# Encoder-decoder layer on one core: short blocks' exponentials queued after the copies, a block's first unit turned head by head, the next rows' norm on ScalarE, and token sums in three parts

## The chip, the cores and the metric

The kernel runs on one core of a Trainium2 chip. The metric is device microseconds of one execution; the number before is the median of three runs, 2858.91 us (2858.62 to 2859.53). Engines are named as the profile names them: PE (TensorE matmul), PEld (its weight load), DVE (VectorE), ACT (ScalarE), POOL (GpSimd), SP (the queue that issues DMAs).

## What is computed

One pre-norm encoder layer on a short source (2 x 77 tokens), and one pre-norm decoder layer on 2 x 2048 tokens, width 512, 16 heads of 32, feed-forward width 2048, all float32. Cut to the decoder, where nearly all the work is:

```
y  = tgt                                   # (2, 2048, 512)
yn = ln(y, n1)
y  = y + mha(yn, yn, sa, bias = rel_self + causal)     # softmax over 16 heads
y  = y + mha(ln(y, n2), memory, ca, bias = rel_cross)  # memory: 77 tokens a batch
h  = ln(y, n3)
y  = y + relu(h @ ff1.T + b1) @ ff2.T + b2
```

`ln` is the layer norm over the 512 columns; `mha` scales scores by 1/sqrt(32), adds the bias, takes the softmax over the keys and multiplies by the values.

## The kernel before

**Blocks and units.** A batch has four blocks of 512 query rows (m = 0 to 3), eight blocks in all. In the first part of the program (to about 1750 us) each block runs its causal self-attention in 16 units: four groups g of four heads, times four tiles t of 128 query rows. A unit's number of key tiles is m*4 + t + 1, so the units of m = 0 are the short ones (1 to 4 key tiles) and those of m = 3 the long ones (13 to 16). Beside a unit run the jobs of a list by unit (`jobs`, `light`, `ahead`, `late`, lines 905 to 943): the projections of queries, keys and values, the output projection of the block before, the layer norm of the next block's rows, and, in the m = 0 block of batch 0, the whole encoder in stages; in the m = 0 block of batch 1, the cross-attention of the first block.

**A unit's steps.** `scores` (line 354) multiplies queries and keys of four heads into four PSUM banks (line 371, four heads on four row groups of the array), and DVE copies them out with a running maximum (lines 380, 387) and takes the row's negated maximum `nm` (line 397). ACT takes the exponential of each head in place and its sum (line 402); for m = 0 the four are issued at once, for m of 1 and more they are put in a list, `late_exps`, from which `exps(k)` issues k at chosen places. `turn` (line 411) transposes the 128 x 128 pieces on PE (line 425), four to a PSUM bank, and copies each bank out, half of them on DVE (line 429) and half on ACT (line 431). For m = 0 a bank holds the pieces of one head, for other blocks the pieces of four heads for one key tile. `values` (line 436) multiplies the copies with the values (line 442).

**The order of the work** is written out by hand (`manual_schedule`, the main loop of lines 1511 to 1536), and every engine runs its own list in order. For a unit n the loop issues: the scores and exponentials of n that are still missing; the norm's statistics that are due (`ahead`); `turn` of a pair of pieces of n; the next unit's list (`slot`); scores of n + 2; one or two late exponentials; `values` of the pair. The scores' banks, the transposes' banks, the jobs' banks and the norm's bank come from one ring of seven, taken in program order (`bank`, line 179).

**The norm of the next rows.** For four units in the middle of a block (lines 933 to 937), one tile a unit: `norm_stats` (bn_stats, bn_aggr, plus epsilon on DVE, the power -1/2 on POOL, lines 281 to 285), `norm_center` (subtract the mean, times rstd, on DVE, 128 x 512, line 291), and a unit later `norm_turn` (four transposes into one bank, line 303, and four 128 x 128 evictions with scale and bias on DVE, line 310). The rows of the very first block are done ahead of everything, with `apart` set, three of their four evictions on ACT (line 308).

**Feed-forward and cross-attention** (from about 1750 us). Each of the eight blocks runs 56 slots (`ff_slot`, line 1378): 28 of the first product and 28 of the second, both as seven products of quarter matrices on sums and differences of the quarters. Four differences of the normed tokens, T1 to T4, are made on POOL in `sums_n` (line 1239) in slot 0; the products (the table `ONE`, line 1173) use T2 from slot 4, T1 from slot 6, T3 from slot 8, T4 from slot 12. A generator `cross` (line 1439) runs the next block's cross-attention beside these slots: in slots 0 to 3 the statistics of its four tiles (POOL lines 743 and 744), two slots later each tile's centring on ACT (line 750) and an addition on POOL (line 751), two slots after that the transposes (line 756) and four evictions on ACT (line 759).

Of the kernel before, what the change touches and what calls it, by code (L numbers as in the profile page):

```python
# [10 lines left out]
F32 = mybir.dt.float32  # L11
AF = mybir.ActivationFunctionType
ALU = mybir.AluOpType
# [4 lines left out]
P = 128  # L18
# [4 lines left out]
HC = P // HD  # L23
# [31 lines left out]
def tile_encoder_decoder(ctx: ExitStack, tc: tile.TileContext, ins, out):  # L55
    nc = tc.nc
# [20 lines left out]
    def vec(name, i):  # L77
        c = _COL[name] + i
        return vecs[:, c : c + 1]
# [78 lines left out]
    with (  # L158
# [20 lines left out]
        def bank():  # L179

            i = count["bank"] % count["banks"]
            count["bank"] += 1
            return psum[:, i, :]

        def in_turn(what, tile):
            i = count[what] % tile.shape[1]
            count[what] += 1
            return tile[:, i, :]

        def rows4(r):  # L190
            return slice(r * HD, (r + 1) * HD)
# [85 lines left out]
        def norm_stats(b, m, t):  # L277
            x1 = xs[b, m, t]
            st = sm.tile([P, 6], F32, name="bnst", tag="bnst")
            mv = sm.tile([P, 2], F32, name="bnmv", tag="bnmv")  # L280
            nc.vector.bn_stats(st, x1)
            nc.vector.bn_aggr(mv, st)
            rs = sm.tile([P, 2], F32, name="rstd", tag="rstd")
            nc.vector.tensor_scalar_add(rs[:, 0:1], mv[:, 1:2], EPS)  # L284
            nc.gpsimd.tensor_tensor(rs[:, 1:2], rs[:, 0:1], mhalf[:, 0:1], ALU.pow)  # L285
            xs[b, m, t] = x1, mv, rs

        def norm_center(b, m, t):
            x1, mv, rs = xs[b, m, t]
            xs[b, m, t] = x1  # L290
            nc.vector.tensor_scalar(x1, x1, mv[:, 0:1], rs[:, 1:2], ALU.subtract, ALU.mult)

        def norm_turn(b, m, t, apart=False):
            xn = xs.pop((b, m, t))
            if t == 0:
                nTs[b, m] = nTt
            nT = nTs[b, m]

            pts = [bank()] * NC
            if apart:  # L300
                pts[0] = bank()
            for c in range(NC):
                nc.tensor.transpose(pts[c][:, ts(c, P)], xn[:, ts(c, P)], ident)
            for c in range(NC):
                d, pt = nT[:, c, ts(t, P)], pts[c]
                sc, bi = vec("dec_n1_s", c), vec("dec_n1_b", c)
                if apart and c:
                    nc.scalar.activation(d, pt[:, ts(c, P)], AF.Identity, bias=bi, scale=sc)
                else:
                    nc.vector.tensor_scalar(d, pt[:, ts(c, P)], sc, bi, ALU.mult, ALU.add)  # L310
# [16 lines left out]
        units = [(b, m, g, t) for b in range(B) for m in range(NMB) for g in range(NC) for t in range(TB)]  # L327
# [14 lines left out]
        def probabilities(n):  # L342
            w = (units[n][1] + 1) * MB
            at = END - HC * w if n % 2 else 0
            return [pp[:, at + r * w : at + (r + 1) * w] for r in range(HC)]

        late_exps = []

        def exps(k):

            for _ in range(min(k, len(late_exps))):
                late_exps.pop(0)[1]()

        def scores(n, k0, kn):
            b, m, g, t = units[n]
            i = m * TB + t
            if k0 == 0:
                state[n] = {
                    "p": probabilities(n),
                    "mx": sm.tile([P, HC, 8], F32, name="mx", tag="mx"),  # L360
                    "nm": sm.tile([P, HC], F32, name="nm", tag="nm"),
                    "col": 0,
                }
                if t == 0:
                    sums_of[b, m, g] = sm.tile([P, TB, HC], F32, name="sums", tag="sums")
            st = state[n]
            last = k0 + kn == i + 1
            q = qTs[b, m, g]
            banks = [bank() for _ in range(HC)]
            for r in range(HC):  # L370
                nc.tensor.matmul(  # L371
                    banks[r][:, : kn * P], q[rows4(r), ts(t, P)], kT[rows4(r), g, k0 * P : (k0 + kn) * P],
                    start=True, stop=True,
                )
            far = max(0, kn - 2) if last else kn
            col = st["col"]
            for r in range(HC):
                p, s, c = st["p"][r], banks[r], col
                if far:
                    nc.vector.tensor_scalar(  # L380
                        p[:, k0 * P : (k0 + far) * P], s[:, : far * P], 1.0, None, ALU.mult, ALU.max,
                        accum_out=st["mx"][:, r, c : c + 1],
                    )
                    c += 1
                if last:
                    w = (kn - far) * P
                    nc.vector.tensor_tensor_reduce(  # L387
                        p[:, (i + 1) * P - w : (i + 1) * P], s[:, far * P : kn * P],
                        biases[b, m, g][:, r, 2 * P - w :], 1.0, LOWEST, ALU.add, ALU.max,
                        accum_out=st["mx"][:, r, c : c + 1],  # L390
                    )
                    c += 1
            st["col"] = c
            if not last:
                return

            nc.vector.tensor_reduce(st["nm"], st["mx"][:, :, :c], AX.X, ALU.max, negate=True)  # L397
            for r in range(HC):
                p, nm, to = st["p"][r][:, : (i + 1) * P], st["nm"][:, r : r + 1], sums_of[b, m, g][:, t, r : r + 1]

                def run(p=p, nm=nm, to=to):
                    nc.scalar.activation(p, p, AF.Exp, bias=nm, accum_out=to)  # L402

                if m:
                    late_exps.append((n, run))
                else:
                    run()

        got = {}

        def turn(pieces):

            first = units[pieces[0][0]][1] == 0
            loads = []
            for n, k0, kn in pieces:
                ks = range(k0, k0 + kn)
                if first:
                    loads += [[(n, k, r) for k in ks] for r in range(HC)]
                else:
                    loads += [[(n, k, r) for r in range(HC)] for k in ks]  # L420
            for o, load in enumerate(loads):
                pt = bank()
                pts = in_turn("pts", pts_all).rearrange("p (x q) -> p x q", q=P)
                for x, (n, k, r) in enumerate(load):
                    nc.tensor.transpose(pt[:, ts(x, P)], state[n]["p"][r][:, ts(k, P)], ident)  # L425
                    got[n, k, r] = pts[:, x, :]
                w = len(load) * P
                if o % 2 if first else o >= (len(loads) + 1) // 2:
                    nc.vector.tensor_copy(pts[:, : len(load), :], pt[:, :w])  # L429
                else:  # L430
                    nc.scalar.copy(pts[:, : len(load), :], pt[:, :w])  # L431
                if o == min(3, len(loads) - 1):
                    exps(1)
            exps(1)

        def values(n, k0, kn):
            b, m, g, t = units[n]
# [473 lines left out]
        for x, (b, m) in enumerate(blocks):  # L911
            u = x * NU
            first = m == 0
# [172 lines left out]
        gp, ve = nc.gpsimd, nc.vector  # L1086
# [14 lines left out]
        def minus(engine, out, a, b):  # L1101
            engine.tensor_tensor(out, a, b, ALU.subtract)  # L1102
# [130 lines left out]
        def of_n(name):  # L1233
            if name[0] == "T":
                return n_sums[:, int(name[1]) - 1]
            r, c = int(name[0]) - 1, int(name[1]) - 1
            return nTt[:, 2 * r : 2 * r + 2, ts(c, TOK)]

        def sums_n():
            minus(gp, of_n("T1"), of_n("12"), of_n("11"))  # L1240
            minus(gp, of_n("T2"), of_n("22"), of_n("T1"))
            minus(gp, of_n("T3"), of_n("22"), of_n("12"))
            minus(gp, of_n("T4"), of_n("21"), of_n("T2"))


        sets = [[high[:, (4 * a + k) * D : (4 * a + k + 1) * D] for k in range(4)] for a in range(2)]
# [130 lines left out]

        def ff_slot(s):
            x, n = divmod(s, per)
            if n == 0:  # L1380
                sums_n()
            k = n - FIRST + 4
            if 0 <= k < 4 * len(TWO):
                sums_h(k // 4, k % 4)
            if n < FIRST:
                first_product(n)
            else:
                second_product(x, (n - FIRST) // 4, (n - FIRST) % 4)
            feed(used[0] + len(w_ring))
            after.pop(s, lambda: None)()  # L1390
            if FIRST <= n < FIRST + TB:
                new_y(x + 2, n - FIRST)
# [118 lines left out]
        while i < len(stream):  # L1511
            n = stream[i][0]
# [91 lines left out]
```

## Time and profile before

| | before |
|---|---|
| median of three runs | 2858.91 us |
| the profiled execution | 2861.14 us, of which 2859.2 us from its first to its last instruction |
| PE busy | 2811.5 us (98%), 25950 matmuls |
| DVE, ACT, POOL busy | 1924.1 us (67%), 1395.4 us (49%), 782.0 us (27%) |
| chain that ended last | PE 89%, DVE 4%, ACT 3%, POOL 2% |
| mean granted PE clock | 0.991 of full speed |

A matmul's record lasts longer than the distance to the next one's start, so a PE that is busy in the table may still stand behind a wait; the distance between starts in the timeline shows it. Lines of the form "L425 <- ACT pp L402" name who ended a wait, and a number in square brackets is the time that the engine stood idle before a row.

### The profile page before, as it was taken

The page shows a single profiled execution, that of the slowest core. Times are in us where ns is not written, and L with a number is a line of the kernel's source. Part 1 is how long each engine was busy: PE and PEld are TensorE (multiplying, and loading weights), DVE is VectorE, ACT ScalarE, POOL GpSimd, SP SyncE. Part 2 cuts the span into 40 slices and gives each one's busy share as a digit, 9 for nine tenths or more (in the row PEclk, how much of TensorE's full clock was granted, in tenths as well). Part 3 has the DMA queues.
Part 4 walks back from the last instruction along what each step waited for, and adds up shares of the span by engine and source line. Part 5 has one row for each costly group of instructions (what it writes and reads, how often), then busy time and mean ns, then how long its engine had stood idle before and what let it go on. Part 6 is the DMA issues. An engine that isn't in the chain of part 4 may idle for free.

```text
span 2859.2 us, 65017 instructions
## 1 busy us (share of the span) xinstructions
PE 2811.5 (98%) x25950; PEld 2070.5 (72%) x25950; DVE 1924.1 (67%) x5416; ACT 1395.4 (49%) x2639; POOL 782.0 (27%) x669
## 2 busy tenths in 40 slices
PE   9899999999999999999999999999999999999998
PEld 5557666666666556666666677888888888888888
DVE  4667688878987677788878885464545555555545
ACT  3344455556666446555556676434344434344431
POOL 0100050200000201120100002282838383737355
PEclk9899999999999999999999999999999999999999
DMA  6413343401112411232401014464647464645466
GB/s 171 117 36 123 120 140 100 122 20 30 36 47 67 118 49 57 82 101 68 123 20 32 24 55 145 151 198 118 199 122 200 139 190 126 188 133 185 119 203 192
DMA packets 252641, 319.10 MB, mean 112 GB/s; under 512 B 29568, under 2 KB 142512, under 8 KB 252210
## 3 DMA queue, kind: packets, MB, share of 16 engines
q1 hardware_dynamic: 252338, 314.93, 37.1%
q8 instruction: 205, 3.36, 0.5%
q14 instruction: 98, 0.80, 0.1%
HBM read 274.91 MB, written 39.95 MB: 110 GB/s over the span
## 4 chain that ended last, share of the span: by engine, by line
PE 89%; DVE 4%; ACT 3%; POOL 2%; issue 1%; DMA 1%; SPq 0%; POOLq 0%; DVEq 0%; ACTq 0%
PE psum L425 17%; PE psum L1346 11%; PE psum L1317 11%; PE psum L371 11%; PE psum L442 9%; PE psum L215 4%; PE psum L239 4%; PE psum L828 4%; PE psum L251 4%; PE psum L226 3%; PE psum L1419 3%; PE psum L811 2%; PE psum L781 1%; ACT pp L402 1%; PE psum L819 1%
## 5 line engine op out<-in xcount | busy, mean ns | idle before, releaser
L402 ACT ACTIVATE pp<-pp,nm 128x128 f32<-128x128 f32 (+15 forms) x512 | 611.9, 1201 | 264.2 <-DVE nm L397 263.9
L380 DVE TENSOR_SCALAR_CACHE_REDUCE pp<-psum 128x512 f32<-128x512 f32 (+3 forms) x1024 | 559.4, 591 | 61.7 <-PE psum L371 60.2
L425 PEld LDWEIGHTS psum<-ident,pp 128*128 128x128 f32 x4352 | 477.2, 142 | 111.1 <-DVE pp L380 51.3
L425 PE MATMUL psum<-ident,pp 128*128 128x128 f32 x4352 | 540.1, 279 | 8.7 <-DVE mx L387 3.8
L431 ACT COPY pts<-psum 128x512 f32<-128x512 f32 (+3 forms) x592 | 297.9, 574 | 471.3 <-PE psum L425 376.8
L429 DVE COPY pts<-psum 128x512 f32<-128x512 f32 (+2 forms) x544 | 330.0, 660 | 69.4 <-PE psum L425 69.1
L371 PE MATMUL psum<-kT,q 32*128 32x512 f32 (+3 forms) x2560 | 362.3, 579 | 6.9 <-ACT pts L431 4.3
L442 PEld LDWEIGHTS psum<-pts,vv 128*32 128x32 f32 x8704 | 227.3, 110 | 125.7 <-issue 117.3
L1346 PEld LDWEIGHTS psum<-pp 128*128 128x128 f32 x2560 | 295.8, 192 | 17.4 <-issue 11.4
L1346 PE MATMUL psum<-pp 128*128 128x128 f32 x2560 | 306.4, 276 | 1.9 <-POOL pp L1102 1.6
L442 PE MATMUL psum<-pts,vv 128*32 128x128 f32 x8704 | 280.7, 276 | 0.7 <-ACT pts L431 0.5
L1102 POOL TENSOR_TENSOR pp<-pp 128x512 f32<-128x512 f32 x155 | 209.7, 1370 | 120.0 <-DMA pp<-in_dec_ff_wT_dram 100.4
L1317 PE MATMUL psum<-vv,pp 128*128 128x256 f32 x1024 | 238.5, 381 | 0.0
L371 PEld LDWEIGHTS psum<-kT,q 32*128 32x128 f32 x2560 | 125.1, 184 | 143.6 <-issue 88.5
L1317 PEld LDWEIGHTS psum<-vv,pp 128*128 128x128 f32 x1024 | 189.8, 190 | 26.3 <-issue 1.9
L387 DVE CUSTOM_DVE_ANT_0 pp<-psum,bias 128x256 f32<-128x256 f32 (+1 forms) x512 | 196.0, 411 | 16.3 <-PE psum L371 16.3
L285 POOL TENSOR_TENSOR rstd<-rstd,mhalf 128x1 f32<-128x1 f32 x32 | 18.2, 570 | 664.3 <-DVE rstd L284 664.3
L1330 DVE TENSOR_TENSOR kT<-kT,psum 128x512 f32<-128x512 f32 x96 | 65.7, 686 | 194.4 <-PE psum L1317 193.9
L1317 PE MATMUL psum<-nT,pp 128*128 128x256 f32 x768 | 173.4, 379 | 0.0
L1333 ACT ACTIVATE kT<-kT,vecs 128x256 f32<-128x256 f32 x192 | 86.9, 500 | 167.9 <-DVE kT L1330 167.8
L1317 PEld LDWEIGHTS psum<-nT,pp 128*128 128x128 f32 x768 | 145.3, 190 | 22.6 <-issue 3.5
L805 POOL TENSOR_TENSOR oT<-oT,cri 128x1232 f32<-128x1232 f32 x28 | 67.7, 2418 | 283.3 <-DVE cri L800 258.4
(191 smaller groups left out, 3712.3 us busy)
## 6 DMA issues: line engine op xcount, KB each, us to landing
pp<-w_d SPq DMA_DIRECT2D x520, 256.0 KB, 3.0
pp<-in_dec_ff_wT_dram SPq DMA_DIRECT2D x112, 256.0 KB, 3.8
wqk<-in_dec_sa_in_wT_dram SPq DMA_DIRECT2D x64, 256.0 KB, 4.0
bias<-tzg SPq DMA_DIRECT2D x128, 128.0 KB, 3.7
wbig<-in_dec_sa_in_wT_dram SPq DMA_DIRECT2D x8, 1024.0 KB, 6.6
vv<-in_enc_ff_wT_dram SPq DMA_DIRECT2D x8, 1024.0 KB, 5.5
wbig<-in_dec_sa_out_wT_dram SPq DMA_DIRECT2D x8, 1024.0 KB, 6.6
vv<-y SPq DMA_DIRECT2D x32, 256.0 KB, 5.8
```

Of the source, the lines that this page charges most:

```text
L215: nc.tensor.matmul(mm, w[:, c, :], nTs[b, m][:, c, :], start=(c == 0), stop=(c == NC - 1))
L371: nc.tensor.matmul(banks[r][:, : kn * P], q[rows4(r), ts(t, P)], kT[rows4(r), g, k0 * P : (k0 + kn) * P], start=True, stop=True,)
L380: nc.vector.tensor_scalar(p[:, k0 * P : (k0 + far) * P], s[:, : far * P], 1.0, None, ALU.mult, ALU.max, accum_out=st["mx"][:, r, c : c + 1],)
L387: nc.vector.tensor_tensor_reduce(p[:, (i + 1) * P - w : (i + 1) * P], s[:, far * P : kn * P], biases[b, m, g][:, r, 2 * P - w :], 1.0, LOW ...
L402: nc.scalar.activation(p, p, AF.Exp, bias=nm, accum_out=to)
L425: nc.tensor.transpose(pt[:, ts(x, P)], state[n]["p"][r][:, ts(k, P)], ident)
L429: nc.vector.tensor_copy(pts[:, : len(load), :], pt[:, :w])
L431: nc.scalar.copy(pts[:, : len(load), :], pt[:, :w])
L442: nc.tensor.matmul(ot[rows4(r), t, :], vv[:, k, ts(g * HC + r, HD)], got.pop((n, k, r)), start=(k == 0), stop=(k == i),)
L1102: engine.tensor_tensor(out, a, b, ALU.subtract)
L1317: nc.tensor.matmul(mm[:, ts(f, TOK)], a[:, c, ts(f, P)], b[:, c, :], start=fresh and f == 0 and c == 0, stop=c == 1, skip_group_check=True,)
L1346: nc.tensor.matmul(psum[:, bank_i, ts(col, P)], lhs[:, c, :], w[:, c, :], start=fresh and k in (0, 3) and c == 0, stop=c == 3, skip_group_ ...
```

## The change

Four edits, in the words of the code:

- In blocks m = 0 the exponentials go into `late_exps` as in the other blocks; `turn` issues one after its last transposed bank and then up to four more (`exps(HC if first else 1)`), so that on ACT they stand behind the unit's copies.
- In the unit g = 0, t = 0 of every block, `turn` fills its banks by head, as m = 0 does everywhere.
- For every block but the first, `norm_center` becomes an ACT activation with scale rstd and bias -mean*rstd; the bias is one more POOL instruction of one column in `norm_stats`; and all four evictions of `norm_turn` go to ACT.
- `sums_n` makes T1 and T2 in slot 0, T3 in slot 4 and T4 in slot 6.

The order of instructions on PE and on SP is the same in both programs, but for the transposes of those first units.

```diff
@@ norm_stats, norm_center, norm_turn
-            rs = sm.tile([P, 2], F32, name="rstd", tag="rstd")
+            rs = sm.tile([P, 3], F32, name="rstd", tag="rstd")
             nc.vector.tensor_scalar_add(rs[:, 0:1], mv[:, 1:2], EPS)
             nc.gpsimd.tensor_tensor(rs[:, 1:2], rs[:, 0:1], mhalf[:, 0:1], ALU.pow)
+            if (b, m) != (0, 0):
+                nc.gpsimd.tensor_scalar(rs[:, 2:3], mv[:, 0:1], rs[:, 1:2], -1.0, ALU.mult, ALU.mult)
             xs[b, m, t] = x1, mv, rs
...
-            nc.vector.tensor_scalar(x1, x1, mv[:, 0:1], rs[:, 1:2], ALU.subtract, ALU.mult)
+            if (b, m) != (0, 0):
+                nc.scalar.activation(x1, x1, AF.Identity, bias=rs[:, 2:3], scale=rs[:, 1:2])
+            else:
+                nc.vector.tensor_scalar(x1, x1, mv[:, 0:1], rs[:, 1:2], ALU.subtract, ALU.mult)
...
-                if apart and c:
+                if c or not apart:
                     nc.scalar.activation(d, pt[:, ts(c, P)], AF.Identity, bias=bi, scale=sc)
@@ scores, turn
-                if m:
-                    late_exps.append((n, run))
-                else:
-                    run()
+                late_exps.append((n, run))
...
             first = units[pieces[0][0]][1] == 0
+            by_head = first or units[pieces[0][0]][2:] == (0, 0)
...
-                if first:
+                if by_head:
                     loads += [[(n, k, r) for k in ks] for r in range(HC)]
                 else:
                     loads += [[(n, k, r) for r in range(HC)] for k in ks]
...
-            exps(1)
+            exps(HC if first else 1)
@@ sums_n, ff_slot
-        def sums_n():
-            minus(gp, of_n("T1"), of_n("12"), of_n("11"))
-            minus(gp, of_n("T2"), of_n("22"), of_n("T1"))
-            minus(gp, of_n("T3"), of_n("22"), of_n("12"))
-            minus(gp, of_n("T4"), of_n("21"), of_n("T2"))
+        def sums_n(n):
+            if n == 0:
+                minus(gp, of_n("T1"), of_n("12"), of_n("11"))
+                minus(gp, of_n("T2"), of_n("22"), of_n("T1"))
+            elif n == 4:
+                minus(gp, of_n("T3"), of_n("22"), of_n("12"))
+            elif n == 6:
+                minus(gp, of_n("T4"), of_n("21"), of_n("T2"))
...
-            if n == 0:
-                sums_n()
+            sums_n(n)
```

## The prediction

> **What bounds the kernel now.** I read the profile in this order: the busy shares and the chain that ended last, PE's own waits, the granted clock by stretches, then the timeline around the longest waits. PE is busy 98% of 2859.2 us and has 89% of the chain, so a step pays only where it shortens a wait of PE or keeps PE's clock up. PE's waits, the longest in total (us in total, times, longest):
>
> ```profile
> PE psum L756 <- ACT xt L750: 7.2, 12, 1.1
> PE psum L371 <- ACT pts L431: 4.3, 4, 1.4
> PE psum L425 <- DVE mx L387: 3.8, 6, 2.0
> PE psum L425 <- ACT pp L402: 3.7, 5, 1.2
> PE psum L781 <- ACT pts L431: 3.7, 2, 3.1
> PE psum L756 <- ACT pts L750: 3.6, 6, 1.1
> PE psum L560 <- ACT pts L431: 3.2, 1, 3.2
> ```
>
> All waits of this view together are under 45 us; what else a change of order can win hides inside PE's overlapping records, and shows in the distances between starts. The second cost is the clock. By stretches of the trace (length, busy time of PE, PEld, DVE, ACT, POOL, then the granted clock):
>
> ```profile
> 95.00:107.00 12.00, 8.62 (x90) 7.47 (x90) 10.25 (x33) 7.71 (x22) 5.52 (x5) 0.57 0.23 43
> 113.00:130.00 17.00, 14.17 (x65) 7.29 (x63) 12.67 (x54) 7.26 (x26) 3.12 (x3) 0.50 0.19 66
> 515.00:523.00 8.00, 7.01 (x75) 4.71 (x74) 5.92 (x16) 7.42 (x12) 1.09 (x2) 0.79 0.52 133
> 645.00:653.00 8.00, 8.00 (x36) 6.12 (x33) 6.41 (x23) 2.76 (x4) 0.00 (x0) 0.57 0.00 0
> 1034.00:1045.00 11.00, 7.88 (x42) 4.63 (x40) 6.66 (x20) 3.66 (x10) 0.00 (x0) 0.69 0.17 49
> 1500.00:1510.00 10.00, 10.00 (x41) 7.22 (x40) 8.41 (x32) 3.40 (x5) 0.00 (x0) 0.66 0.00 0
> ```
>
> Length times missing clock gives 5.2, 8.5, 1.7, 3.4, 3.4 and 3.4 us, 25.6 us in all. The four stretches in batch 0's and 1's short blocks and at 515 us stand at waits that this change touches; the two at 645 and 1500 us stand where DVE empties score banks without a pause, which it does not touch.
>
> **Token sums in parts.** The timeline of one feed-forward block's start:
>
> ```profile
> 1915.03 1.27 POOL L1102 TENSOR_TENSOR vv<-nT 128x512 f32<-128x512 f32 x1
> ...
> 1918.84 1.27 POOL L1102 TENSOR_TENSOR vv<-nT,vv 128x512 f32<-128x512 f32 x1
> ...
> 1920.71 0.27 POOL L744 TENSOR_SCALAR crs<-cmv,crs 128x1 f32<-128x1 f32 x1
> ...
> 1921.02 0.81 ACT L750 ACTIVATE xt<-vv,crs 128x512 f32<-128x512 f32 x1 [2.37 <-POOL crs L744]
> ...
> 1921.88 0.66 PE L756 MATMUL psum<-ident,xt 128*128 128x128 f32 x4 [1.09 <-ACT xt L750]
> ...
> 1924.77 0.66 PE L756 MATMUL psum<-ident,xt 128*128 128x128 f32 x4 [0.50 <-ACT xt L750]
> ...
> 1927.35 0.66 PE L756 MATMUL psum<-ident,pts 128*128 128x128 f32 x4 [0.19 <-ACT pts L750]
> ```
>
> POOL makes T1 to T4 in a row (4 x 1.23 us from start to start); the second tile's rstd stands behind them, ACT's centring waits 2.37 us for it, and PE's transposes wait for that. With T3 and T4 moved out, rstd is ready 2.5 us sooner (1918.5). ACT can then centre from 1918.6, where it ends a relu, not 1921.02. Next is ACT itself: until the fourth tile's centring it has a relu pair (0.79), two sets of evictions (1.38 each), two more centrings (0.70, the last ending 0.81 after its start) and a copy (0.47), which put that end at 1925.4 instead of 1927.3. So 1.9 us of the 2.3 us that PE loses here (eight products take 1.73 us from start to start; the three stretches took 2.98, 2.39 and 2.08) go. Six blocks have this, at 140 us distance: **-11.4 us**. Bounds: -13.6 (all of it) and 0. T3 is needed in slot 8 and T4 in slot 12; by the same rows POOL has them at about 1925 and 1928, slot 8 begins near 1927, slot 12 at 1935, so I count no new wait; without that margin a late sum costs at most its 1.27 us a block.
>
> **Copies ahead of exponentials (m = 0).** The longest wait:
>
> ```profile
> 95.39 0.72 ACT L402 ACTIVATE pp<-pp,nm 128x512 f32<-128x512 f32 x1 [5.98 <-DVE nm L397]
> ...
> 97.52 0.71 ACT L402 ACTIVATE pp<-pp,nm 128x512 f32<-128x512 f32 x1
> ...
> 98.22 0.83 ACT L431 COPY pts<-psum 128x384 f32<-128x384 f32 x2
> ...
> 98.73 1.19 PE L560 MATMUL psum<-pp 32*77 32x77 f32 x26 [3.16 <-ACT pts L431]
> ```
>
> PE stands 3.16 us for a bank whose copy is queued on ACT behind four exponentials of the unit after, and these behind DVE's maximum. After the change one exponential is still ahead (the one that the loop issues after the scores), three are behind: the copies come 3 x 0.71 = 2.1 us sooner. The same at 1034 us (L781, 3.1 us): 2.1. The waits of 1.36 and 0.92 us at 115 and 124 us (L371) and 0.58 at 1013 us (L781) are shorter than their three exponentials (0.49 or 0.60 each, 0.39 at 1013 us) and go. **-7.1 us**; bounds -9.1 (those waits whole) and the loss of the slower rival below. The three exponentials are next needed by the following `turn`, head by head. Cover: between two turns of short units PE has its jobs (a projection's four products 1.72 us, two of them 3.6), scores (0.2 to 0.5) and values (0.1 to 0.4); the least, without a projection, is some 1.2 us, and then a head's transposes 0.1 to 0.4 us apart. That is about level with three exponentials, so nothing is counted.
>
> **Norm on ACT.** Per tile DVE hands over four evictions (1.36 us together) and a centring (0.54): 1.9 us; ACT takes four (1.38) and a centring (0.70 from start to start, 0.82 long by the same operation at L750): 2.1 us. There are 28 tiles. Where it helps: at 111 us PE waits 2.03 us for DVE's L387, with these 1.9 us just ahead on DVE, and smaller waits of that kind (0.56, 0.48) stand near: -2.5. At 515 and 1373 us DVE's maximum is late, ACT has stood idle for 7.90 us before the exponential that it releases, and copies and scores wait behind: 1.9 each, -3.8. **-6.3 us**, bounds -9 and 0. Elsewhere ACT's 2.1 us stand beside the output projection of the block before (two jobs, 3.6 us of PE), while ACT waits for PE (idle 5.88 us before 767.7 us, 7.70 before 276 us, 4.39 before 498 us): nothing; without that cover 2.1 us a tile. The added wait is ACT's on POOL: 0.57 + 0.32 us (L285, L744) after DVE's statistics, with a whole `turn` in between; behind it stand the next unit's copies. POOL's 28 more instructions are 9 us of an engine that is idle 73%. The row buffers are loaded by the same SP instructions in the same order; a centring that ends later only eats slack of a unit.
>
> Where it costs: in short blocks the evictions now stand behind three exponentials, and the ring of seven banks comes round to the norm's bank. At 98 us the bank would be free at about 100.4 us (copies to 96.9, three exponentials 2.1, evictions 1.4), not 98.5, and the next scores want it: I charge 2. In batch 1's short block ACT also carries the first cross-attention's evictions (958 to 970 us without a pause): 0.5 + 1.0. With 0.5 for the rest: **+4.0 us**, bounds 0 and +8 (1 us for each of eight tiles in short blocks).
>
> [...]
>
> **First unit by head.** At 632 and 1489 us the first unit of m = 3 waits for the fourth head's exponential (1.24 of the 3.7 us, each time), because every bank takes all four heads. By head, twelve transposes (0.11 each, 1.3 us) come first: -1.1 each, **-2.2 us**; bounds -2.5 and +2. The price is eight banks where there were five: ACT copies four of 384 columns (0.36) for three of 512 (0.48), the same; DVE four of 256 (0.34) for two of 512 (0.61), +0.15 a block.
>
> **Clock.** I let the falls at 515 and 1034 us go with their waits, **-5.1 us**, and leave the others; bounds -12 (half of the early two as well) and +3 (a new fall).
>
> [...]
>
> **Sum.** -11.4 - 7.1 - 6.3 + 4.0 - 2.2 - 5.1 = -28.1 us, made against the profiled execution (2861.14 us, 1.9 of it outside the span). The median is 2.2 below that execution; the same saving from it: 2858.9 - 28.1 = **2831 us**.
>
> **Rivals.**
> - Only the sums and the turn pay: in the short blocks the bank waits of the evictions eat what copies and DVE give, the clock falls stay. 2858.9 - 11.4 - 2.2 = 2845 us. For it: DVE is busy 10.25 of 12 and 12.67 of 17 us there, so another wait may end last.
> - Everything opens up: the early clock falls shrink too. -13.6 - 9.1 - 9 - 2.5 - 12 = -46: 2813 us. Against it: PE's clock fell where no wait was long.
> - Slower: in the 32 short units the three exponentials behind the copies become what the next turn waits for. They last 3 x (0.39 + 0.50 + 0.60 + 0.71)/4 = 1.65 us on average, 53 us in all; with the copies' gain void, 2858.9 - 28.1 + 7.1 + 53 = 2891 us. It beats the rest from 21/32 = 0.66 us a unit. Against it: half of the units have a projection in between (1.7 us or more).
> - The edits do nothing on the path (PE's waits move to other lines): 2859 us.
>
> **Chances.** Forecast 0.60 (2820 to 2842), sums and turn only 0.16, everything 0.10, no change 0.06, slower 0.08. The range 2813 to 2850 takes in the first three. Faster by over 0.2% (5.7 us; less cannot be told from no change) 0.86, within 0.06, slower 0.08.
>
> **What would show it.** Right: PE's waits on L750 fall from 10.8 to under 3 us; those on ACT's copies from 11.7 to under 5; L425 on L402 to under 2; clock 1.00 at 515 and 1034 us. Wrong: new waits of PE's L425 on the exponentials in m = 0, or of L371 on the norm's evictions; the clock lower than 0.88 from 100 to 200 us.

## The result, and the profile after

The changed kernel takes **2827.75 us** (median of four runs, 2825.34 to 2830.27) against 2859.22 of the kernel before on the same chip: ratio 0.9889, 95% interval [0.9872, 0.9906], 31.5 us less. The four runs lie in two pairs, near 2825.5 us (mean granted clock 0.997) and near 2830.0 us (0.996), and the profiled execution is one of the latter: 2830.27 us, span 2828.5, mean granted clock 0.996 (before: 2859.2, 0.991). The diff moves the line numbers: L371 is now L376, L380 L385, L387 L392, L397 L402, L402 L407, L425 L428, L431 L434, L310 L313, L560 L563, L744 L747, L750 L753, L756 L759, L781 L784, L1102 L1105; the centring on ACT is L294.

The page after, busy time of each engine, and the chain that ended last:

```profile
PE 2796.6 (99%) x25950; PEld 2062.6 (73%) x25950; DVE 1872.9 (66%) x5288; ACT 1454.0 (51%) x2785; POOL 787.9 (28%) x697
...
PE 93%; DVE 3%; ACT 1%; issue 1%; DMA 1%; POOL 1%; SPq 0%; POOLq 0%; ACTq 0%; DVEq 0%
```

DVE is 51 us shorter and ACT 59 us longer, as the norm's move says; PE's share of the chain rose from 89% to 93%. PE's own waits after (us in total, times, longest):

```profile
PE psum L428 <- ACT pp L407: 2.8, 5, 0.9
PE psum L376 <- ACT nT L313: 2.7, 1, 2.7
PE psum L376 <- DVE pp L385: 2.6, 5, 1.0
...
PE psum L563 <- ACT pts L434: 1.1, 1, 1.1
PE psum L784 <- ACT pts L434: 1.0, 1, 1.0
```

The waits on the feed-forward's centring (L750 before, 10.8 us in two groups) are gone. The two waits of 3.1 us for copies are 1.1 and 1.0. The second row is new: scores that wait 2.7 us for the norm's evictions on ACT. The stretches (length, busy PE, PEld, DVE, ACT, POOL, then the granted clock):

```profile
95.00:107.00 12.00, 7.94 (x88) 6.56 (x87) 8.72 (x29) 8.95 (x23) 6.42 (x8) 0.72 0.25 45
113.00:130.00 17.00, 14.91 (x133) 9.29 (x129) 12.52 (x56) 11.79 (x37) 2.27 (x2) 1.00 0.36 115
500.00:520.00 20.00, 20.00 (x197) 12.61 (x196) 15.12 (x40) 12.41 (x23) 4.08 (x6) 1.00 0.35 91
640.00:650.00 10.00, 10.00 (x95) 6.08 (x93) 6.93 (x31) 7.88 (x12) 0.00 (x0) 1.00 0.01 2
1020.00:1032.00 12.00, 10.79 (x68) 6.35 (x60) 9.33 (x31) 3.68 (x10) 1.15 (x1) 0.72 0.17 46
1483.00:1493.00 10.00, 10.00 (x42) 7.16 (x43) 8.90 (x34) 2.65 (x5) 0.00 (x0) 0.66 0.01 2
```

A fall is a stretch in which the granted clock is 0.50 of full speed, as the clock records of both traces give it. Three of six falls are gone (113, 515 and 645 us in the old times); of the three that remain, the first shrank from 10.2 to 6.8 us.

Where the 30.7 us between the two spans went: DVE takes the negated maximum (L397, now L402) once a unit, 128 times in either program, so the difference of these starts, from unit to unit, places each microsecond.

| place | after minus before, us |
|---|---|
| start, to 57 us (no edit reaches it) | +0.7 |
| batch 0, short block from 57 us (with 20.5 us less of lowered clock) | -8.5 |
| batch 0, m = 2: norm units -1.3, +1.4, -1.3; fall at 519 us gone -1.6 (with small steps -2.6) | -2.6 |
| batch 0, m = 3: first unit -1.0, fall at 645 us gone -1.3 | -2.3 |
| batch 1, short block and its end, to 1050 us (of it +1.7 at 958 us) | -1.2 |
| batch 1, m = 2: norm units -1.3, +1.35, -1.4 | -1.1 |
| batch 1, m = 3: first unit -1.0, then -0.5 | -1.5 |
| after the attention: six blocks, 2.2 to 2.6 each | -14.2 |

The m = 1 blocks and the norm units of m = 3 moved by 0.15 us at most.

One feed-forward block's start after the change, where before the second rstd came at 1920.7 and PE waited for the centring:

```profile
1898.55 1.28 POOL L1105 TENSOR_TENSOR vv<-nT 128x512 f32<-128x512 f32 x1
...
1899.90 1.27 POOL L1105 TENSOR_TENSOR vv<-nT,vv 128x512 f32<-128x512 f32 x1
...
1901.77 0.27 POOL L747 TENSOR_SCALAR crs<-cmv,crs 128x1 f32<-128x1 f32 x1
...
1902.07 0.81 ACT L753 ACTIVATE xt<-vv,crs 128x512 f32<-128x512 f32 x1
...
1904.16 0.60 PE L759 MATMUL psum<-ident,xt 128*128 128x128 f32 x4
...
1907.72 0.84 ACT L753 ACTIVATE pts<-vv,crs 128x512 f32<-128x512 f32 x1
...
1908.62 0.66 PE L759 MATMUL psum<-ident,pts 128*128 128x128 f32 x4
```

Add 16.48 us to come to the old times: rstd is ready at 1918.52 and the centring starts at 1918.55 (worked out: 1918.5 and 1918.6). PE's sets of transposes start 2.17, 2.16 and 2.30 us apart (1.73 of products, 0.44 of transposes) with no wait in brackets; T3 stands behind the last rstd, at 1907.4. The fourth centring ends at 1908.56 and its transposes start 0.06 us later.

### The profile page after: what moved, and what is told of

Same layout as the page of the kernel before. It is cut to its first block, busy times and chain, and to the rows that moved or that the text cites. A ratio compares the mean times of both kernels' runs of the same rounds, so it can differ in the third digit from the quotient of the medians.

```text
span 2828.5 us, 65166 instructions
## 1 busy us (share of the span) xinstructions
PE 2796.6 (99%) x25950; PEld 2062.6 (73%) x25950; DVE 1872.9 (66%) x5288; ACT 1454.0 (51%) x2785; POOL 787.9 (28%) x697
## 4 chain that ended last, share of the span: by engine, by line
PE 93%; DVE 3%; ACT 1%; issue 1%; DMA 1%; POOL 1%; SPq 0%; POOLq 0%; ACTq 0%; DVEq 0%
PE psum L428 17%; PE psum L1323 14%; PE psum L1352 12%; PE psum L376 11%; PE psum L445 9%; PE psum L215 4%; PE psum L831 4%; PE psum L251 4%; PE psum L239 4%; PE psum L226 3%; PE psum L1424 3%; PE psum L814 2%; DVE pp L385 1%; PE psum L784 1%; PE psum L822 1%; PE psum L546 1%
## 5 line engine op out<-in xcount | busy, mean ns | idle before, releaser
L407 ACT ACTIVATE pp<-pp,nm 128x128 f32<-128x128 f32 (+15 forms) x512 | 612.7, 1204 | 219.7 <-DVE nm L402 219.2
L385 DVE TENSOR_SCALAR_CACHE_REDUCE pp<-psum 128x512 f32<-128x512 f32 (+3 forms) x1024 | 559.4, 591 | 61.7 <-PE psum L376 60.2
L428 PEld LDWEIGHTS psum<-ident,pp 128*128 128x128 f32 x4352 | 472.9, 141 | 111.8 <-DVE pp L385 53.1
L428 PE MATMUL psum<-ident,pp 128*128 128x128 f32 x4352 | 536.6, 277 | 9.2 <-ACT pp L407 2.8
L434 ACT COPY pts<-psum 128x512 f32<-128x512 f32 (+3 forms) x598 | 298.8, 571 | 437.6 <-PE psum L428 333.4
L432 DVE COPY pts<-psum 128x512 f32<-128x512 f32 (+3 forms) x556 | 330.8, 648 | 68.6 <-PE psum L428 68.5
L376 PE MATMUL psum<-kT,q 32*128 32x512 f32 (+3 forms) x2560 | 356.6, 576 | 6.0 <-ACT nT L313 2.7
L1105 POOL TENSOR_TENSOR pp<-pp 128x512 f32<-128x512 f32 x155 | 209.5, 1368 | 111.7 <-DMA pp<-in_dec_ff_wT_dram 90.8
L376 PEld LDWEIGHTS psum<-kT,q 32*128 32x128 f32 x2560 | 122.9, 183 | 141.2 <-issue 87.9
L392 DVE CUSTOM_DVE_ANT_0 pp<-psum,bias 128x256 f32<-128x256 f32 (+1 forms) x512 | 196.0, 411 | 17.0 <-PE psum L376 17.0
```

Source lines behind the costliest of these rows:

```text
L376: nc.tensor.matmul(banks[r][:, : kn * P], q[rows4(r), ts(t, P)], kT[rows4(r), g, k0 * P : (k0 + kn) * P], start=True, stop=True,)
L385: nc.vector.tensor_scalar(p[:, k0 * P : (k0 + far) * P], s[:, : far * P], 1.0, None, ALU.mult, ALU.max, accum_out=st["mx"][:, r, c : c + 1],)
L392: nc.vector.tensor_tensor_reduce(p[:, (i + 1) * P - w : (i + 1) * P], s[:, far * P : kn * P], biases[b, m, g][:, r, 2 * P - w :], 1.0, LOW ...
```

## The experiments

Each kernel is the one before, or the changed one, with the edit shown. "Placed" numbers are differences by unit as in the table. **Theory:** each edit takes away a wait of its own at the places worked out, so gains are found where they were put, and the clock's falls follow the waits. **Rivals:** one edit's relief carries the short blocks and the others are superfluous; or falls of the clock come and go by another rule.

### The four parts one by one

**Token sums in parts** (`sums_alone`): the `sums_n` part of the diff.

> The kernel before with the token sums in parts alone. Theory (POOL's order was the whole cause of the three stretches, and ACT's centrings end just in time): six feed-forward blocks x 2.26 us = -13.6 us, all of it after 1750 us, the attention unchanged. By the prediction's price (ACT's own chain keeps 0.35 us a block): -11.4 us. Rival (the gain needs the other edits, or T3 and T4 come late): 0 to -5 us, with new waits of PE in slots 8 and 12.

2845.10 us, ratio 0.9953 [0.9940, 0.9965], -13.9 us. Placed: -13.2 after the attention. The theory holds; ACT's chain keeps nothing back. But the attention, whose code is the same as before, moved as well: -2.1 at 663 us, +1.6 at 537 us, and -1.2 in batch 0's short block. The two stretches in this kernel:

```profile
515.00:523.00 8.00, 7.29 (x68) 4.64 (x69) 4.70 (x13) 6.15 (x12) 1.78 (x2) 0.65 0.54 131
645.00:653.00 8.00, 8.00 (x42) 4.93 (x40) 7.76 (x26) 4.44 (x6) 0.00 (x0) 1.00 0.00 0
```

Before, these rows had a clock of 0.79 and 0.57. The same instructions lost the fall at 645 us and had a longer one at 517 us (6.83 instead of 3.41 us). So a fall is not tied to its place alone. Nor does it keep its start: the fall at 95.96 us before starts 1.7 us later here (the stretch from 95 to 107 us reads 0.72, before 0.57: 6.7 us of half clock for 10.3). What sets the start is not shown.

**Late exponentials in m = 0** (`exps_alone`):

```diff
-                if m:
-                    late_exps.append((n, run))
-                else:
-                    run()
+                late_exps.append((n, run))
...
-            exps(1)
+            exps(HC if first else 1)
```

> The kernel before with the late exponentials of m = 0 alone (copies ahead of them). Theory (the queue on ACT is what PE stood for in the short blocks, and the second clock fall of batch 0's block came from those waits): -6 to -8 us by 170 us, -2 to -4 us in batch 1's short block, elsewhere nothing: about -9 us. Rival 1 (DVE's relief by the norm carries batch 0's block): -4.2 us, the two long waits alone, and the second clock fall stays. Rival 2 (the next turn waits for the exponentials): slower.

2849.44 us, ratio 0.9966 [0.9954, 0.9979], -9.6 us. PE's waits for these copies in this kernel (L557 is L560 before, L778 L781):

```profile
PE psum L557 <- ACT pts L428: 1.1, 1, 1.1
PE psum L778 <- ACT pts L428: 1.0, 1, 1.0
```

3.16 and 3.1 us became 1.1 and 1.0: the three exponentials' 2.1 us, as worked out. PE's shorter waits for copies at 115, 124 and 1013 us are gone. Placed: -5.2 in batch 0's short block from 57 us, with 6.8 us less of lowered clock there, and -4.3 at 1021 to 1050 us, where the fall at 1038 us is gone; elsewhere -0.5 and -0.4 early in the m = 1 blocks, +1.6 for a new fall at 1367 us and -2.3 at 1519 us for one that is gone. No wait of the next turn for an exponential appeared. The theory holds for the waits. Its number for batch 0 (6 to 8) was not reached, and its cause for the second fall there is not shown: that fall shrank from 17.1 to 13.7 us and stayed, as rival 1 had it.

**Norm on ScalarE** (`norm_alone`): the parts of the diff in `norm_stats`, `norm_center` and `norm_turn`.

> The kernel before with the next rows' norm on ScalarE alone. Theory (in the long blocks it saves 1.3 us at three of four norm units of m = 2 and gives 1.4 back at the fourth; in batch 0's short block it saves the wait for DVE's maximum at 111 us, 2 us): m = 2 -2.7 and -1.3 us, batch 0's short block -2, batch 1's 0 to +2: about -5 us. Rival (the relief of DVE is what opened batch 0's short block): -8 us there by 170 us, -11 in all. Slower rival (ACT's evictions delay the copies while the exponentials stand ahead of them): +2 to +4 us in the short blocks.

2848.46 us, ratio 0.9963 [0.9949, 0.9977], -10.6 us: more than the theory's 5, near the rival's 11. Placed: -6.2 in batch 0's short block from 57 us, -2.7 and -1.2 in the m = 2 blocks, +1.7 at 982 us, -1.5 at 1050 us, and three steps of falls (-2.3 at 1519 us, +1.7 for a new one at 168 us; -1.6 at 537 us is within the -2.7). PE's wait of 2.03 us for DVE's maximum at 111 us is gone (the longest of that kind is now 0.7). The waits for copies are untouched (L565 and L786 are L560 and L781 before):

```profile
PE psum L786 <- ACT pts L436: 3.7, 2, 3.1
PE psum L565 <- ACT pts L436: 3.2, 1, 3.2
```

So the move of the norm is a cause of its own in batch 0's short block, as large as the queue on ACT. Its lowered clock there fell from 27.3 to 13.7 us, and how much of the 6.2 us is shorter waits and how much clock was not separated. Alone, the norm and the exponentials give 11.3 us there, together 8.5 (each with its falls); I put the 2.8 us between down to waits that both take away.

**First unit by head** (`head_alone`): `by_head` in `turn`.

> The kernel before with the first unit of each block turned head by head alone. Theory (each of the two long blocks' first units gives 1.0 us, and the clock fall at 645 us goes with it for 1.3 us): -2.3 us in batch 0 and -1.5 us in batch 1, -3.8 us in all, nothing in m = 1 and m = 2. By the prediction's price: -2.2 us. Rival (the fall at 645 us comes and goes by where the block stands in time, so it stays here): -1.0 and -1.5 us.

2856.28 us, ratio 0.9988 [0.9980, 0.9997], -2.8 us. Placed: -0.98 at 646 and -0.98 at 1502 us, exactly the changed kernel's; the rest of the steps are falls that stayed away (-1.3 at 663, -1.5 at 1519 us). That the fall at 645 us went with its edit is not settled: `sums_alone` lost it without this edit. For it speaks that none of the ten profiles of kernels with this edit has that fall, and three of the four without it have.

The four medians add up to -36.8, the whole gave -31.5. Of the difference 2.8 us is what the two edits give less together in batch 0's short block; the rest I put down to falls, which each execution has in its own places; it was not separated further.

### The whole again, and without the norm

`after_again` is the changed kernel itself, profiled once more.

> The changed kernel once more, nothing altered, for a second profile. [...] Rival (a fall belongs to its place in the program): the same three falls, of 6.8 us each, and a span within 0.5 us of 2828.5.

2829.22 us, span 2827.4. The same three falls at the same places; the span is 1.1 us shorter, all of it before 57 us. By the falls this speaks for the rival, though the span is 1.1 us off, not 0.5. But one more execution that came out alike does not show that the falls belong to their places: in `sums_alone` unchanged code at 645 us lost its fall (granted clock 1.00, before 0.57).

`no_norm`: the changed kernel without the norm's three edits.

> The changed kernel with the next rows' norm back on VectorE (sums, late exponentials and the turn by head kept). Theory (beside the late exponentials the norm on ScalarE gives 3 us in batch 0's short block and 2.7 + 1.2 us in the m = 2 blocks, and costs 1.7 us in batch 1's short block): 5 us slower than the changed kernel without the clock falls, 3 to 7 with them: about 2833 us. Rival 1 (the two are independent, so all of the 10.6 us that the norm gave alone come back): 2838 us. Rival 2 (its costs in the short blocks eat its gain): 2826 to 2828 us, nothing changed.

2835.68 us (ratio 0.9913 [0.9898, 0.9928]), 7.9 us above the changed kernel's median, but 5.2 us by the two profiled spans. Placed against the changed kernel: +4.2 in batch 0's short block from 57 us, with 13.7 us more of lowered clock there; +2.65 and +2.8 in m = 2 (1.6 of each a fall); -3.5 in batch 1's short block and its end (1.7 of it where the fall at 1024 us is gone); -1.0 for a fall. The spans give the theory's 5, the medians lie between it and rival 1's 10.6: the norm pays beside the late exponentials, and costs in batch 1's short block.

### Taking the change's own costs away

`rows11`: in batch 1's short block the norm stays on VectorE.

```diff
-            if (b, m) != (0, 0):
+            if (b, m) not in ((0, 0), (1, 1)):
...
-                if c or not apart:
+                if (c or not apart) and (b, m) != (1, 1):
```

> The changed kernel, with the norm of one block's rows (batch 1, m = 1, made beside batch 1's short block) on VectorE as before; the other six blocks' stay on ScalarE. Theory (there ScalarE carries the cross-attention's evictions too and has no pause from 945 to 963 us, so the norm's work there is path): the 1.73 us lost at 958 us come back: -1.7 us against the changed kernel, and up to -2 more if the fall at 1024 us goes. Rival (DVE is as full there as ScalarE and the wait returns on DVE's lines): 0.

2826.49 us (ratio 0.9882 [0.9868, 0.9897]). Its four runs (2825.33 to 2826.74) lie inside the changed kernel's, so the medians do not tell the two apart. Placed against the changed kernel, in its times: -1.76 at 970 us and -1.6 at 1037 us (the fall at 1024 us is 3.4 us long, not 6.8). The place in the changed kernel, ACT's queue and PE's wait behind it:

```profile
955.09 0.71 ACT L407 ACTIVATE pp<-pp,nm 128x512 f32<-128x512 f32 x1
...
955.79 1.49 ACT L313 ACTIVATE nT<-psum,vecs 128x128 f32<-128x128 f32 x4
957.16 0.82 ACT L294 ACTIVATE xt<-xt,rstd 128x512 f32<-128x512 f32 x1
957.87 1.51 ACT L762 ACTIVATE pp<-psum,vecs 128x128 f32<-128x128 f32 x4
...
959.43 0.77 PE L428 MATMUL psum<-ident,pp 128*128 128x128 f32 x5 [0.89 <-ACT pp L762]
```

The norm's 1.49 and 0.82 us stand ahead of the cross-attention's evictions, and PE waits for these. The theory's 1.73 us are there.

`exp0`: in m = 0 no exponential is issued after the scores.

```diff
-            exps(2 if units[n][1] == 1 else 1)
+            exps((0, 2, 1, 1)[units[n][1]])
```

> The changed kernel, with no exponential issued after the scores in blocks m = 0 (all four of a unit go behind the copies of the unit before it). Theory (the one exponential that still stands ahead of the copies waits for DVE's maximum, and the copies with it): the waits of 2.03 us at 94.9 us and 1.31 us at 1022.8 us go, -2 to -3.3 us. Rival 1 (four exponentials in a row behind the copies make the next turn wait for the first head): PE's L428 waits for L407 in the short units, 0.4 to 0.7 us each in up to 32 units: slower by up to 10 us. Rival 2 (PE waits for the scores' banks there, not for the copies): 0.

2823.98 us (ratio 0.9876 [0.9859, 0.9892]). Placed against the changed kernel, in its times: -1.0 in batch 0's short block, -0.5 at 958 us, -3.1 at 1037 us (no fall there), -1.0 at 1503 us (a fall less). No line of PE waiting for exponentials grew, so rival 1 is out. Of the theory's two waits that at 1022.8 us is gone, together with the fall behind it; the two were not separated. At 95 us only 1.0 us was won. The wait there went over to DVE: its copies stand behind the norm's statistics (L432, 1.3 us), and the scores' wait for the evictions is 1.9 us instead of 2.7:

```profile
95.34 0.72 ACT L407 ACTIVATE pp<-pp,nm 128x512 f32<-128x512 f32 x1 [2.01 <-DVE nm L402]
...
98.17 1.48 ACT L313 ACTIVATE nT<-psum,vecs 128x128 f32<-128x128 f32 x4
...
99.71 0.80 PE L376 MATMUL psum<-kT,q 32*128 32x128 f32 x4 [1.93 <-ACT nT L313]
```

The row says what to do next: ACT stands idle for 2.01 us before the exponentials, and the evictions that PE then waits for would fit there.

### Putting the repairs together

`best1`: `rows11` and `exp0`, and every centring in a list of its own:

```diff
-                    light[u - NU + 6 + t].append(lambda b=b, m=m, t=t: norm_center(b, m, t))
+                    behind[u - NU + 6 + t].append(lambda b=b, m=m, t=t: norm_center(b, m, t))
...
+            if ends:
+                for f in behind[n + 1]:
+                    f()
```

(the last three lines follow the `exps` after the scores).

> The changed kernel with three repairs: no exponential after the scores in m = 0; the rows of batch 1, m = 1 normed on VectorE; and every centring issued behind the exponential that follows the scores, not ahead of it. Theory (each repair takes away a wait of its own): against the changed kernel's profile -1.4 us by the first repair, -1.7 by the second, and by the third the 1.41 and 1.35 us that the two m = 2 blocks gave back at their second norm unit: -5.9 us without the clock falls, and less if falls go too: about 2819 to 2822 us. Rival for the third (the head's exponential is late anyway, since ScalarE works from the maximum on without a pause): the 1.4 us stay in both blocks and the time is 2822 to 2824 us.

2827.11 us (ratio 0.9887 [0.9871, 0.9904]): the expectation failed. Placed against `exp0`: +2.1 at the start, which no edit touches (a fall at 12 us); in each m = 2 block -1.1, then +0.7 and +0.7; in batch 1's short block +2.2, where PE's L308 waits up to 1.7 us for the centring that VectorE now does too late. The m = 2 rows of the changed kernel tell why the third repair must be for the first centring alone:

```profile
470.65 1.46 ACT L407 ACTIVATE pp<-pp,nm 128x1408 f32<-128x1408 f32 x1
...
473.24 0.81 ACT L294 ACTIVATE xt<-xt,rstd 128x512 f32<-128x512 f32 x1 [1.04 <-POOL rstd L287]
...
473.96 1.45 ACT L407 ACTIVATE pp<-pp,nm 128x1408 f32<-128x1408 f32 x1
```

The first centring stands ahead of the fourth head's exponential and waits 1.04 us itself, and PE's transposes wait for that head (0.94 us):

```profile
475.56 2.62 PE L428 MATMUL psum<-ident,pp 128*128 128x128 f32 x22 [0.94 <-ACT pp L407]
```

The second and third centrings fill 2.3 and 2.9 us in which ACT waits for the next maximum.

`best2` adds, for m = 0, the evictions ahead of the exponentials and the statistics behind the copies; `best3` is the same with the norm of all seven blocks on ScalarE:

```diff
             turn(pair)
+            if short:
+                for f in front[n + 1]:
+                    f()
+                exps(HC)
+                for f in ahead[n + 1]:
+                    f()
```

(`front` holds the short blocks' `norm_turn`, `turn` itself issues none of their exponentials, and `ahead` runs before `turn` in the other blocks only.)

> As best1, and in blocks m = 0 the norm's four evictions stand ahead of the unit's exponentials on ScalarE, and the norm's statistics behind the copies on VectorE. Theory (ScalarE stands idle 2.0 us for DVE's maximum before the exponentials at 95.3 us, time enough for the evictions of 1.48 us, whose bank PE waits for at 99.7 us; and DVE's copies at 96.2 us come 1.0 us sooner without the statistics ahead): the waits of 1.93 and 1.31 us there go, -2 to -4 us against best1 by 170 us. Rival (the exponentials, 1.5 us later, are what the next turn waits for): no gain, with PE's L428 waiting for the exponentials in batch 0's norm units, 0 to +4 us.

> As best2, with the norm of all seven blocks' rows on ScalarE. Theory (with the evictions ahead of the exponentials ScalarE still has no pause in batch 1's short block, so VectorE is the better place there): 1 to 2 us slower than best2, at 958 us. Rival (the loss of 1.73 us came from the evictions' place behind the exponentials, not from ScalarE's load): same as best2 within 0.3 us.

`best2` 2825.61 us (0.9884 [0.9869, 0.9898]), `best3` 2821.99 us (0.9869 [0.9855, 0.9884]). Against `exp0`, batch 0's short block gives -2.1 and -2.9 us from 57 us on: the theory's 2 to 4. In batch 1's short block `best2` loses 2.6 us and `best3` gains 1.2. `best3` is neither slower than `best2`, as the theory had it, nor the same, as the rival had it, but 3.6 us faster. So ScalarE's load was not what cost 1.7 us at 958 us: with the whole norm on ScalarE and its place in the queue changed, that loss is gone, and ScalarE is the better engine there too (the late centring on VectorE is part of `best2`'s loss). Whether the evictions' place or the centring's did it these two cannot say, since `best3` moved both; `best4` tells.

`best4` is `best3` with only the first centring beside an m = 2 block late; the centrings beside the short blocks thereby go back ahead as well:

```diff
-                    behind[u - NU + 6 + t].append(lambda b=b, m=m, t=t: norm_center(b, m, t))
+                    (behind if m == 3 and t == 0 else light)[u - NU + 6 + t].append(lambda b=b, m=m, t=t: norm_center(b, m, t))
```

> As best3, with one change: only the first of the four centrings beside an m = 2 block stands behind the exponential that follows the scores, the other three as in the changed kernel. Theory (the first centring stood ahead of the last of four exponentials that ScalarE works on without a pause, 1.2 us of path; the second and third fill pauses of 2.3 and 2.9 us that ScalarE has before the next maximum, and moved behind they stand ahead of the copies, 0.7 us of path each): against best3 -1.4 us in each m = 2 block, so -2.8 us: a span of about 2817.5 us with the same clock falls, a median of 2819 us. Rival (the 0.7 us come from the first centring's move, which delays the rows' first transposes): against best3 no change, 2822 us.

**2819.69 us** (2818.36 to 2821.34), ratio 0.9857 [0.9841, 0.9874]; span 2817.2. Placed against `best3`: -0.7 and -0.7 in each m = 2 block, -2.75 in all, as expected. The two spans differ by 3.1 us; their other steps were not forecast and nearly cancel: -1.3 at the start, -0.7 and -1.4 for falls that are shorter or gone, +1.7 for a new fall at 159 us, and +1.6 in batch 1's short block. That the span came within 0.3 us of the expected 2817.5 is thus partly luck. Every run of it is below every run of the changed kernel (2825.34 at the least), so it beats both, by some 41 and 8 us. ACT at 468 us, in order, and then the evictions at 93 us that now fill ACT's wait for the maximum:

```profile
467.53 1.46 ACT L407 ACTIVATE pp<-pp,nm 128x1408 f32<-128x1408 f32 x1
...
468.98 0.80 ACT L294 ACTIVATE xt<-xt,rstd 128x512 f32<-128x512 f32 x1
470.19 2.06 ACT L434 COPY pts<-psum 128x512 f32<-128x512 f32 x4 [0.41 <-PE psum L428]
```

```profile
93.36 1.51 ACT L313 ACTIVATE nT<-psum,vecs 128x128 f32<-128x128 f32 x4 [0.69 <-PE psum L308]
...
94.75 0.73 ACT L407 ACTIVATE pp<-pp,nm 128x512 f32<-128x512 f32 x1
```

The +1.6 us in batch 1's short block stand at 945 and 953 us, with no fall near. PE's transposes there in `best3`, then in `best4`, with ACT's rows before the second wait:

```profile
945.76 1.55 PE L428 MATMUL psum<-ident,pp 128*128 128x128 f32 x12
...
953.03 2.10 PE L428 MATMUL psum<-ident,pp 128*128 128x128 f32 x16
```

```profile
945.60 0.88 PE L428 MATMUL psum<-ident,pp 128*128 128x128 f32 x6 [0.73 <-ACT kT L231]
...
953.41 1.53 PE L428 MATMUL psum<-ident,pp 128*128 128x128 f32 x12 [0.81 <-ACT pp L762]
```

```profile
951.16 0.81 ACT L294 ACTIVATE xt<-xt,rstd 128x512 f32<-128x512 f32 x1
951.87 1.49 ACT L762 ACTIVATE pp<-psum,vecs 128x128 f32<-128x128 f32 x4
```

The norm's evictions stand ahead of the exponentials in both kernels. In `best3` the centring follows the cross-attention's evictions (L762) and PE does not wait; in `best4` it stands ahead of them, and the changed kernel's loss is back. So that loss hangs on the centring's place; the evictions' place alone does not take it away. `best4` with these centrings left late was not run; by these rows it should be about 1.6 us faster still, an estimate.

## Why the prediction was right, and where its steps were not

Forecast 2831 us, measured 2827.75: right in sign and nearly in size, inside the forecast's own 2820 to 2842. By place it is less close. The forecast's terms add up to -4.9 us in batch 0's short block, -4.6 in batch 1's, -5.5 in the m = 2 blocks, -2.2 in m = 3 and -11.4 after the attention; the profiles gave -8.5, -1.2, -3.7, -3.8 and -14.2. Each place is off by 1.6 to 3.6 us and the errors largely cancel, so that the sum is only some 3 us off is partly luck. By its terms:

- **Token sums, -11.4:** the mechanism was right, the size 13.2 (placed, alone) to 13.9 (median). The mis-sized term is what ACT's own chain was to keep: 0.35 us a block. The end of the fourth centring was put at 1925.4 us, but the terms listed for it, added from 1918.6 us on, give only 1924.8; it ended at 1925.04 in old times, just when PE came to it. T3 and T4 made no wait.
- **Copies ahead, -7.1:** right for the waits. The two long ones lost 2.1 us each, as worked out, and the three shorter ones went. What that is worth in time is not shown to the microsecond: the placed -5.2 and -4.3 hold two shortened or vanished falls as well.
- **Norm on ACT, -6.3 and +4.0:** net -2.3 was too small: taking the norm out again costs 7.9 us by the medians, 5.2 by the profiled spans. Three steps. The gain in batch 0's short block was put at 2.5 less 2, with the clock left as it was: `no_norm` places it at 4.2 net, with 13.7 us of lowered clock in it that the forecast did not count. In m = 2 the 1.9 us a block are 2.6 less 1.4 = 1.2: the loss of 1.4 at the first centring was not seen, since "nothing" was said of all norm units where ACT waits for PE; this one stands ahead of an exponential. In batch 1's short block 1.5 was charged for ScalarE's load and 1.73 measured, at the place named; but the load was not the reason, since in `best3` ScalarE carries the same work without that loss, with the centring later in its queue. The charge of 2 at 98 us is there as a wait of 2.7 us.
- **First unit by head, -2.2:** 0.98 twice, right.
- **Clock, -5.1:** not confirmed. Lowered clock fell from 51.2 to 20.5 us in all; two thirds of this lie in batch 0's short block, where its share in the -8.5 was not separated. Of the two falls that were to go, that at 515 us went (1.6 us for 1.7), that at 1034 us is still there at 1024 us; the one at 113 us, left standing in the sum, went, and that at 645 us too. That a fall goes with its wait failed as a step: with the wait at 1038 us cut from 3.1 to 1.0 us the fall stayed here and went in `exps_alone`; and in `sums_alone` the fall at 645 us went with no edit near it. With both 3.1 us waits cut to 1.1 and 1.0, one of the two falls shrank from 10.2 to 6.8 us and the other stayed 6.8 us long.

Of the signs named beforehand, these came: waits on L750 10.8 to 0; on copies 11.7 to under 5; clock 1.00 at 515 us; as a wrong sign, the wait on the norm's evictions. These did not: L425 on L402 went from 3.7 to 2.8, not under 2 (two waits of 0.4 us went, the two of 1.24 fell to 0.25, and two new ones of 0.9 came in the m = 2 blocks); the clock at 1034 us. The slower rival (late exponentials) never showed: no wait of that kind in the short blocks, and `exp0`, with one exponential more behind the copies, is faster still.

## What to carry to other kernels

Work that fills an engine's idle time is free only if it stands in the queue where the idle time is: of three norm units of an m = 2 block that got the same 0.8 us centring two became 1.3 us shorter and one 1.4 us longer, by one place in the order, and in batch 1's short block the centring's place was worth 1.6 us; so for each instruction moved, read the row behind it on its new engine and what that row waits for. Attribute small differences by unit from two traces, not by medians, and take falls of the clock out first. An add-up of parts measured alone (36.8 us here) overstates the whole (31.5), at least in part because two of them remove the same waits.

## What the runs showed of the hardware

- **When the clock fell.** By the clock records the falls before start at 95.96, 113.03, 519.21, 645.51, 1038.04 and 1502.25 us and last 10.24, 17.07, 3.41, 6.83, 6.83 and 6.83 us; after, they start at 99.44, 1024.45 and 1485.25 us and last 6.83 us each. (One more in either runs past the program's end.) The lengths are one to five times the shortest, and the starts within either execution are whole multiples of it apart, to 0.01 us; from run to run they moved (the first by 1.7 us in `sums_alone`). Code that was not changed had a fall at 645 us in one execution (0.57, before) and none in another (1.00, `sums_alone`).
- **What a fall costs:** 3.41 us of half clock cost 1.62 to 1.67 us (517 us in `sums_alone`, 168 in `norm_alone`, 1366 in `exps_alone`), nearly the full half; 6.83 us at 645 and 1502 us cost 2.1 to 2.3 in the old order of the turn and 1.0 to 1.45 in the new one (1477 to 1485 us), not 3.4; there PE's weight loads wait for DVE's emptying of score banks as well (0.3 us before several of them at 643 to 647 us in the kernel before), which I take for the reason.
- **What decides a fall is not the recorded waits alone:** in the 3.41 us before the fall at 519 us PE's records cover 0.71 (2.42 us, before); stretches of that length with 0.68 at the feed-forward's block starts (2.32 us from 1918.68 us) were followed by none; before the fall at 1502 us they cover all of it (3.40 us). This stays open.
